# Layer 0 of a four-layer graph kernel: pinned trips through DRAM, reordered small loads, identity products on TensorE, and row scaling on ScalarE

## The chip, the cores and the metric

The kernel runs on one core of one Trainium2 chip. The metric is the device time of one execution in microseconds (us). Every time below is the median of several executions; the profile is one execution, and its span is some 2 us shorter than the time of the same execution (986.9 against 988.83 us before the change). Engines: PE is TensorE's matmul, PEld its weight load, DVE VectorE, ACT ScalarE, POOL GpSimd, SP the engine that issues most DMAs.

## The reference

`x` has 32 batches of 512 nodes with 128 features, `adj` is 512 by 512 with about one entry in eight set. Four layers follow one another, each `x = x + layer(relu(layernorm(x)))`. Only layer 0 matters here:

```python
def _L0_gnn_ref(input, adj, W, e, bias):
    NEG = -9000000000000000.0
    h0 = jnp.einsum('bnf,fg->bng', input, W[0])
    h1 = jnp.einsum('bnf,fg->bng', input, W[1])
    m = adj > 0
    idx = jnp.cumsum(m.reshape(-1).astype(jnp.int32)) - 1
    vals = e[0][idx].reshape(adj.shape)      # e has 256 entries: later ones clamp to the last
    A = jnp.where(m, vals, jnp.float32(NEG))
    A = jax.nn.softmax(A, axis=1)
    M = jnp.eye(adj.shape[0], dtype=A.dtype)
    out = jnp.einsum('ij,bjg->big', A * M, h0) + jnp.einsum('ij,bjg->big', A * (1.0 - M), h1)
    return out + bias[None, None, :]
# ... layers 1 to 3: Chebyshev hops, message passing, attention
```

The comment on `e` is mine: only the first 256 set entries get a value of their own, and the others get the last value, which is why "e's last value" is treated apart.

## The kernel before

The order of instructions on the four computing engines is fixed by the program. The order of DMA issues in SP's queue is not, unless an issue is wrapped in `keep_in_program_order`; a scheduler places the others (in the kernel before, an issue of tile 5 stands in front of tile 4's return, which then comes at 62.91 us). Layer 0 treats the batches in 16 tiles of two. Tiles 0 to 3 are turned to feature-major form by TensorE; from tile 4 on VectorE transposes 32 by 32 squares and the rest of the turn is a trip through DRAM:

```python
    def turn_steps(h, name, done):
        hb = late.tile([P, NQR, 2, NT, QR], F32, tag="hb", name=f"hb_{name}", bufs=2)
        for b in range(2):
            nc.vector.transpose(hb[:, :, b].rearrange("p j t r -> p t j r"),
                                h[:, b].rearrange("p t (j c) -> p t j c", c=QR))
            yield
        d = bounce.tile([NQR, QR, NQR, 2 * P], F32, tag="d", name=f"d_{name}")
        for i in range(NQR):                      # outward: four issues of 128 KB
            nc.sync.dma_start(d[:, :, i, :].rearrange("j c e -> c j e"),
                              hb[i * QR : (i + 1) * QR].rearrange("c j b t r -> c j (b t r)"))
        hT = feature_major(name)                  # return: one issue of 512 KB
        nc.sync.dma_start(hT.rearrange("p i b n -> p (i b n)"), d.rearrange("j c i e -> (j c) (i e)"))
        done[name] = hT
```

The products of a round r (two tiles) are seven; `p_l_a`, `p_l_c` and `p_l_d` are banks of partial sums. Between them stand the projections of the next round's tiles, `p_g`, which read `hT`:

```python
            if i == 0:
                if C + 2 < NQ:
                    go(turn(C + 2))               # round 1: tile 5
            # ...
            elif i == 1:
                if r == 1:
                    go(squares, 3)
                if more:
                    go(projection(A + 2))         # round 1: p_g of tile 4
            # ...
            elif i == 4:
                if r == 1:
                    go(squares, 3)                # its last step: adjT_d, 4 issues of 256 KB
                if A + 4 < NQ:
                    go(turn(A + 4))               # round 1: tile 6
```

(`squares` writes the transposed adjacency to DRAM, where layer 3 reads it.) The start builds the attention matrix from one-hot products:

```python
    def keep_busy(n):                             # products nobody reads: hold the clock up
        p = bank("p_idle")
        for _ in range(n):
            nc.tensor.matmul(p, upto[:, 0, blk(0)], upto[:, 0, :], start=True, stop=True)

    def masked(t):                                # two passes over each row block, on GpSimd
        nc.gpsimd.tensor_scalar(att[:, t, :], m[:, t, :], -2.0 * NEG, NEG, OP.mult, OP.add)
        nc.gpsimd.tensor_scalar(att[:, t, :], att[:, t, :], elastn, None, OP.max)

    def score_rows(t):
        ph = bank(f"p_first_{t}")
        # ... two products at_row x at_col into ph, six at_row x at_part into p_val

    def scaled_rows(t, scaled=None):              # rows 0 to 2: GpSimd; row 3: ScalarE
        if scaled is None:
            nc.gpsimd.tensor_scalar(split(att[:, t, :]), crossed(us[t]), total[:, t : t + 1], None, OP.mult)
        else:
            scaled(split(att[:, t, :]), crossed(us[t]), total[:, t : t + 1])
        # ... diagonal taken out by two more GpSimd operations
```

## Time and profile before

| | before |
|---|---|
| time | 987.59 us (987.29 to 988.96, 3 runs; 987.97 with a fourth) |
| span of the profile | 986.9 us |
| TensorE busy | 961.6 us, 97% |
| TensorE's two waits for a trip through DRAM | 5.84 and 5.78 us |
| first `p_l_a` of round 0 | 33.17 us |

The page, the waits, the two gaps and SP's queue are shown and read in the prediction below. What it only quotes is the start. TensorE's timeline of the kernel before; the columns are start, duration, engine, line, operation, output and inputs, and count, with the idle time before it and its releaser in brackets:

```profile
19.49 0.59 PE L626 MATMUL p_first<-at_col,at_row 128*128 128x512 bf16 x2
19.92 1.74 PE L630 MATMUL p_val<-at_part,at_row 128*128 128x512 bf16 x6
...
28.43 3.74 PE L425 MATMUL p_g<-w,hT 128*128 128x128 f32 x32
...
33.17 1.99 PE L376 MATMUL p_l_a<-g,attT 128*128 128x256 f32 x8
```

The scores begin at 19.49 us, directly behind other products, and the projections of both tiles of round 0 stand together as 32 products after them. Between 9.09 us and `p_l_a` TensorE never idles for more than 0.46 us at a time; in front of 9.09 it had waited 3.56 us for `p_incl`, the first product that needs the whole adjacency.

### The profile page before, as it was taken

Reading aid. Unit: us, or ns where it says so; the run is one execution under the profiler, and the core shown is the slowest. Engines: PE = TensorE matmul, PEld = TensorE weight load, DVE = VectorE, ACT = ScalarE, POOL = GpSimd, SP = SyncE. Lnnn points to the kernel's source line nnn. Section 1 sums busy time; section 2 is a strip of 40 time slices with the busy share of each in tenths; the row PEclk is TensorE's granted clock in tenths of the full one; section 3 lists DMA queues with packets and bytes.
Section 4 is the critical chain, followed back from the end, with each engine's and each line's share of the span. In section 5 each row is a group of like instructions: output and inputs, shape, how many; then the busy total and the mean of one; then the engine's idle time right before and its main releaser. Section 6 shows DMA issues by size and latency. Waiting matters only on the chain.

```text
span 986.9 us, 15155 instructions
## 1 busy us (share of the span) xinstructions
PE 961.6 (97%) x5463; PEld 784.6 (79%) x5464; DVE 578.3 (59%) x1316; ACT 469.9 (48%) x1052; POOL 443.9 (45%) x489
## 2 busy tenths in 40 slices
PE   7977999999999999999999999999999999999998
PEld 3867999989898988989977777777767776777776
DVE  7666787574455456467568665655664444444444
ACT  4762544352421421555836554554664554445553
POOL 7966588855326724421623434444133322233322
PEclk9988999999999999999999999999999999999999
DMA  9046454154232211234332332223132121121111
GB/s 253 10 118 160 129 163 116 43 139 118 68 115 75 65 50 58 76 95 130 86 110 68 122 107 86 69 82 86 43 88 77 51 72 58 54 76 44 54 33 43
DMA packets 83913, 86.04 MB, mean 87 GB/s; under 512 B 6784, under 2 KB 74624, under 8 KB 83840
## 3 DMA queue, kind: packets, MB, share of 16 engines
q1 hardware_dynamic: 83136, 84.96, 30.7%
q8 instruction: 43, 0.70, 0.3%
q14 instruction: 30, 0.25, 0.1%
q10 hardware_dynamic: 704, 0.13, 0.1%
HBM read 44.17 MB, written 40.89 MB: 86 GB/s over the span
## 4 chain that ended last, share of the span: by engine, by line
PE 87%; POOL 4%; DVE 4%; ACT 2%; issue 1%; DMA 1%; SPq 0%; POOLq 0%; DVEq 0%; ACTq 0%
PE p_av L1107 12%; PE p_score L1092 11%; PE p_l_c L376 8%; PE p_l_d L376 5%; PE p_w L425 5%; PE p_l_a L376 5%; PE p_msgT_c L369 4%; PE p_x1T_c L369 4%; PE p_feat L425 3%; PE p_hv L425 3%; PE p_msgT_d L369 3%; PE p_msgT_a L369 3%; PE p_qkh L1079 3%; PE p_l L425 3%; PE p_g L425 3%; PE p_phi L1062 3%
## 5 line engine op out<-in xcount | busy, mean ns | idle before, releaser
L239 ACT ACTIVATE h<-x,sh,rs 128x128 f32<-128x128 f32 x512 | 209.1, 484 | 58.1 <-DVE sh L228 24.7
L1097 POOL TENSOR_TENSOR ex<-ex,adjTx 128x512 f32<-128x512 f32 x64 | 83.3, 1303 | 206.3 <-ACT ex L1095 206.3
L1093 ACT ACTIVATE ex<-p_score 128x512 f32<-128x512 f32 x128 | 71.8, 587 | 124.6 <-issue 113.0
L1107 PEld LDWEIGHTS p_av<-qkh_hv,ex 128*128 128x128 f32 x1024 | 118.5, 191 | 9.4 <-issue 7.4
L1107 PE MATMUL p_av<-qkh_hv,ex 128*128 128x129 f32 x1024 | 120.1, 275 | 0.8 <-POOL ex L1097 0.8
L1092 PE MATMUL p_score<-qkh_hv,hT 128*128 128x512 f32 x256 | 115.2, 593 | 0.0
L275 DVE STREAM_TRANSPOSE hb_hT<-h 128x512 f32<-128x512 f32 x120 | 81.8, 697 | 35.3 <-ACT h L239 34.9
L1097 DVE TENSOR_TENSOR ex<-ex,adjTx 128x512 f32<-128x512 f32 x64 | 45.4, 710 | 81.7 <-ACT ex L1095 81.7
L219 DVE BATCH_NORM_STATS2 bn<-x 128x6 f32<-128x256 f32 x248 | 89.7, 416 | 0.9
L1092 PEld LDWEIGHTS p_score<-qkh_hv,hT 128*128 128x128 f32 x256 | 46.2, 190 | 46.5 <-issue 45.0
L1095 ACT ACTIVATE ex<-ex 128x512 f32<-128x512 f32 x128 | 76.6, 630 | 1.8
L347 POOL TENSOR_TENSOR rt_feat<-feat,feat 128x256 f32<-128x256 f32 x16 | 11.6, 727 | 137.2 <-ACT feat L1046 137.2
L347 POOL TENSOR_TENSOR rt_w<-w 128x512 f32<-128x512 f32 x16 | 20.3, 1269 | 81.1 <-ACT w L953 81.1
L425 PE MATMUL p_w<-th,x1T 128*128 128x128 f32 x256 | 49.5, 275 | 0.0
L425 PE MATMUL p_w<-th,hs 128*128 128x128 f32 x256 | 49.5, 275 | 0.0
L390 ACT COPY x1T<-p_x1T_a 128x256 f32<-128x256 f32 x16 | 5.9, 369 | 84.3 <-PE p_x1T_a L369 84.3
L425 PE MATMUL p_g<-w,hT 128*128 128x128 f32 x256 | 34.7, 294 | 11.6 <-DMA hT<-d_hT 11.6
L425 PEld LDWEIGHTS p_hv<-vw,hT 128*128 128x128 f32 x256 | 33.6, 192 | 15.3 <-issue 8.1
L1057 POOL TENSOR_TENSOR x<-x,phi2b 128x256 f32<-128x256 f32 x64 | 44.5, 728 | 0.0
L450 ACT COPY g<-p_g 128x512 f32<-128x512 f32 x30 | 17.4, 584 | 56.6 <-PE p_g L425 56.4
L425 PEld LDWEIGHTS p_g<-w,hT 128*128 128x128 f32 x256 | 33.4, 209 | 12.6 <-DMA hT<-d_hT 6.2
L1064 ACT ACTIVATE msgT<-p_phi,phi1b 128x512 f32<-128x512 f32 x32 | 21.7, 678 | 40.8 <-PE p_phi L1063 40.8
(230 smaller groups left out, 2104.9 us busy)
## 6 DMA issues: line engine op xcount, KB each, us to landing
d_hT<-hb_hT SPq DMA_DIRECT2D x240, 128.0 KB
hT<-d_hT SPq DMA_DIRECT2D x60, 512.0 KB
x<-in_x_dram SPq DMA_DIRECT2D x32, 256.0 KB
out_dram<-x SPq DMA_DIRECT2D x31, 256.0 KB
adj_s<-in_adj_dram SPq DMA_DIRECT2D x4, 256.0 KB
adjT_d<-adj_squares SPq DMA_DIRECT2D x4, 256.0 KB
sq<-in_adj_dram SPq DMA_DIRECT2D x4, 256.0 KB
adjTx<-adjT_d SPq DMA_DIRECT2D x4, 256.0 KB
```

The source lines that it names most:

```text
L219: nc.vector.bn_stats(st[:, k].rearrange("p e s -> p (e s)"), xt[q][:, b, t : t + 2, :].rearrange("p t f -> p f t"))
L239: nc.scalar.activation(h[:, b, t, :], xt[q][:, b, t, :], AF.Relu, bias=shift[q][:, i : i + 1], scale=scale[q][:, i : i + 1])
L275: nc.vector.transpose(hb[:, :, b].rearrange("p j t r -> p t j r"), h[:, b].rearrange("p t (j c) -> p t j c", c=QR))
L369: nc.tensor.matmul(p[:, :H], b[:, k, :], a[:, k, :], start=(first and k == 0), stop=(k == 1), skip_group_check=True)
L376: nc.tensor.matmul(p[:, i * 2 * D : (i + 1) * 2 * D], a[:, k, blk(i)], b[:, k], start=(first and i == 0 and k == 0), stop=(k == 1), skip_g ...
L425: nc.tensor.matmul(p[:, blk(t)], hT(t), w, start=(i == 0), stop=(i == len(terms) - 1))
L1057: tc.keep_in_program_order(nc.gpsimd.tensor_add(xi, xi, spread(phi2b, 2)))
L1092: nc.tensor.matmul(ps, hT[:, t, b, :], qkh, start=True, stop=True)
L1093: nc.scalar.activation(ex[:, t, :], ps, AF.Tanh, scale=1.0 / (8.0 * math.sqrt(D)))
L1095: nc.scalar.activation(ex[:, t, :], ex[:, t, :], AF.Exp, scale=8.0)
L1097: eng.tensor_mul(split(ex[:, t, :]), split(ex[:, t, :]), crossed(adjTx[0][:, t, :]))
L1107: nc.tensor.matmul(po[:, i, : D + 1], ex[:, t, blk(i0 + i)], hv[:, t, :], start=(t == 0), stop=(t == NT - 1))
```

## The change

Its intent: close the two gaps of nearly 6 us, and shorten the start by relieving GpSimd. The core of the diff (reordered surroundings and renamings are cut):

```diff
# 1. trips of layer 0 keep their order in SP's queue
         d = bounce.tile([NQR, QR, NQR, 2 * P], F32, tag="d", name=f"d_{name}")
+        hT = feature_major(name)
+        held = tc.keep_in_program_order if name.startswith("hT0") else lambda step: step
         for i in range(NQR):
-            nc.sync.dma_start(d[:, :, i, :]...)
-        hT = feature_major(name)
-        nc.sync.dma_start(hT..., d...)
+            held(nc.sync.dma_start(d[:, :, i, :]...))
+        held(nc.sync.dma_start(hT..., d...))
# 2. loads: e, q and k behind x in SP's queue, not in ScalarE's
-    nc.scalar.dma_start(elast, ...)
-    nc.scalar.dma_start(ecol, ...)
-    qw = load_rows(q_w, "qw", nc.scalar)[:, 0, :]
-    kw = load_rows(k_w, "kw", nc.scalar)[:, 0, :]
+    nc.sync.dma_start(ecol, ...)        # behind x of batches 0 to 3, before w0
+    nc.sync.dma_start(elast, ...)
+    qw = load_rows(q_w, "qw")[:, 0, :]
+    kw = load_rows(k_w, "kw")[:, 0, :]
# 3. the mask: one pass, and e's last value by an identity product
-        nc.gpsimd.tensor_scalar(att[:, t, :], m[:, t, :], -2.0 * NEG, NEG, OP.mult, OP.add)
-        nc.gpsimd.tensor_scalar(att[:, t, :], att[:, t, :], elastn, None, OP.max)
+        nc.gpsimd.tensor_scalar(att[:, t, :], m[:, t, :], -1.0, -NEG, OP.add, OP.mult)
+    for t in range(NT):
+        scores[t] = bank(f"p_later_{t}")
+        nc.tensor.matmul(scores[t], ident16, m[:, t, :], start=True, stop=False)
# 4. the ten small operations that split e into three bf16 parts: moved from the
#    front of the program to behind the second next(early[0]) (same code)
# 5. statistics: two of the four small operations to VectorE; tile 1 as a whole
-            nc.gpsimd.tensor_scalar(sd[:, half], st[:, half, :, 2], 1.0 / D, EPS, OP.mult, OP.add)
+            if whole and b == 0:
+                continue
+            half = slice(0 if whole else 2 * b, 2 * b + 2)
+            nc.vector.tensor_scalar(sd[:, half], st[:, half, :, 2], 1.0 / D, EPS, OP.mult, OP.add)
# 6. order on TensorE: the projection of tile 0 before the first scores
-    go(normal[1])
-    go(turned[0])
+    go(normal[1], 3)
+    go(turned[0])
+    next(project[0])
+    go(normal[1])
# 7. ScalarE scales all four row blocks
-            nc.gpsimd.tensor_scalar(split(att[:, t, :]), crossed(us[t]), total[:, t : t + 1], None, OP.mult)
+        nc.scalar.mul(split(att[:, t, :]), crossed(us[t]), total[:, t : t + 1])
# 8. warming products
-    keep_busy(8)
+    keep_busy(16)
# ... keep_busy(3) becomes 4; the later 2, 4 and 1 go; scores, softmax and projections interleave
# ... round 0: the normalising of tile 2 and the statistics behind it move up a little
```

More of the change, by code (lines that the diff above doesn't have):

```diff
@@ L119, in load_x, with load_rows @@
         return nc.sync.dma_start(xt[b // 2][:, b % 2], x[b].rearrange("(t p) f -> p t f", p=P))
-    def load_rows(ap, name, eng=nc.sync):
+    def load_rows(ap, name):
         o = ap.shape[0] // P
         w = const.tile([P, o, ap.shape[1]], F32, name=name)
-        eng.dma_start(w, ap.rearrange("(o f) g -> f o g", f=P))
+        nc.sync.dma_start(w, ap.rearrange("(o f) g -> f o g", f=P))
         return w
@@ L136 @@
         load_x(b)
+    ecol = const.tile([P, NK], F32, name="ecol")
+    nc.sync.dma_start(ecol, e_l0.rearrange("o (k p) -> p (o k)", p=P))
+    elast = const.tile([P, 1], F32, name="elast")
+    nc.sync.dma_start(elast, bass.AP(tensor=e_l0.tensor, offset=e_l0.offset + NE - 1, ap=[[0, P], [1, 1]]))
+    qw = load_rows(q_w, "qw")[:, 0, :]
+    kw = load_rows(k_w, "kw")[:, 0, :]
     w0 = const.tile([P, 2, D], F32, name="w0")
     nc.sync.dma_start(w0, w_l0.rearrange("o f g -> f o g"))
-    elast = const.tile([P, 1], F32, name="elast")
-    nc.scalar.dma_start(elast, bass.AP(tensor=e_l0.tensor, offset=e_l0.offset + NE - 1, ap=[[0, P], [1, 1]]))
-    ecol = const.tile([P, NK], F32, name="ecol")
-    nc.scalar.dma_start(ecol, e_l0.rearrange("o (k p) -> p (o k)", p=P))
-    qw = load_rows(q_w, "qw", nc.scalar)[:, 0, :]
-    kw = load_rows(k_w, "kw", nc.scalar)[:, 0, :]
     b0 = load_bcast(bias_l0, "b0")
@@ L191, in ln_stats, with early_stats @@
             pass
-    def early_stats(q):
+    def early_stats(q, whole):
         st = stats.tile([P, NT, 2, 3], F32, tag="bn", name=f"bn_{q}", bufs=4)
@@ L201, in early_stats @@
         for b in range(2):
-            half = slice(2 * b, 2 * b + 2)
             for k in range(2 * b, 2 * b + 2):
@@ L206, in early_stats @@
                                    xt[q][:, b, t : t + 2, :].rearrange("p t f -> p f t"))
-            nc.gpsimd.tensor_scalar(sd[:, half], st[:, half, :, 2], 1.0 / D, EPS, OP.mult, OP.add)
+            if whole and b == 0:
+                continue
+            half = slice(0 if whole else 2 * b, 2 * b + 2)
+            nc.vector.tensor_scalar(sd[:, half], st[:, half, :, 2], 1.0 / D, EPS, OP.mult, OP.add)
+            nc.vector.tensor_scalar(sh[:, half], st[:, half, :, 1], -1.0, None, OP.mult)
             nc.gpsimd.tensor_tensor(rs[:, half], sd[:, half], minus_half[:, half], OP.pow)
-            nc.gpsimd.tensor_mul(sh[:, half], st[:, half, :, 1], rs[:, half])
-            nc.gpsimd.tensor_scalar(sh[:, half], sh[:, half], -1.0, None, OP.mult)
+            nc.gpsimd.tensor_mul(sh[:, half], sh[:, half], rs[:, half])
             yield
@@ L278, in turn_steps @@
         d = bounce.tile([NQR, QR, NQR, 2 * P], F32, tag="d", name=f"d_{name}")
+        hT = feature_major(name)
+        held = tc.keep_in_program_order if name.startswith("hT0") else lambda step: step
         for i in range(NQR):
-            nc.sync.dma_start(d[:, :, i, :].rearrange("j c e -> c j e"),
-                              hb[i * QR : (i + 1) * QR].rearrange("c j b t r -> c j (b t r)"))
-        hT = feature_major(name)
-        nc.sync.dma_start(hT.rearrange("p i b n -> p (i b n)"), d.rearrange("j c i e -> (j c) (i e)"))
+            held(nc.sync.dma_start(d[:, :, i, :].rearrange("j c e -> c j e"),
+                                   hb[i * QR : (i + 1) * QR].rearrange("c j b t r -> c j (b t r)")))
+        held(nc.sync.dma_start(hT.rearrange("p i b n -> p (i b n)"), d.rearrange("j c i e -> (j c) (i e)")))
         done[name] = hT
@@ L494 @@
     att = square_tile("att")
-    elastn = prep.tile([P, 1], F32, name="elastn")
-    nc.gpsimd.tensor_scalar(elastn, elast, -1.0, None, OP.mult)
-    ecoln = prep.tile([P, NK], F32, name="ecoln")
-    nc.gpsimd.tensor_scalar(ecoln, ecol, -1.0, None, OP.mult)
-    parts = []
-    for i in range(3):
-        eh = prep.tile([P, NK], BF16, name=f"eh_{i}")
-        nc.gpsimd.tensor_copy(eh, ecoln)
-        part = prep.tile([P, NK], F32, name=f"part_{i}")
-        nc.gpsimd.tensor_copy(part, eh)
-        if i < 2:
-            nc.gpsimd.tensor_sub(ecoln, ecoln, part)
-        parts.append(part)
-    keep_busy(8)
+    ident16 = prep.tile([P, P], F16, name="ident16")
+    nc.gpsimd.tensor_copy(ident16, ident)
+    keep_busy(16)
     for t in range(NT):
@@ L513 @@
                                 accum_out=rc[:, t : t + 1])
-    def masked(t):
-        nc.gpsimd.tensor_scalar(att[:, t, :], m[:, t, :], -2.0 * NEG, NEG, OP.mult, OP.add)
-        nc.gpsimd.tensor_scalar(att[:, t, :], att[:, t, :], elastn, None, OP.max)
+        nc.gpsimd.tensor_scalar(att[:, t, :], m[:, t, :], -1.0, -NEG, OP.add, OP.mult)
     rch = prep.tile([P, NT], F16, name="rch")
     nc.vector.tensor_copy(rch, rc)
-    masked(0)
     pi = bank("p_incl")
@@ L529 @@
                              start=(s == 0), stop=(s == t))
-    p = bank("p_qk_t")
-    nc.tensor.transpose(p[:, blk(0)], qw, ident)
-    nc.tensor.transpose(p[:, blk(1)], kw, ident)
-    qkT = prep.tile([P, 2, D], F32, name="qkT")
-    nc.scalar.copy(qkT, tiles(p)[:, :2, :])
-    keep_busy(3)
-    early = [early_stats(q) for q in range(2)]
+    keep_busy(4)
+    early = [early_stats(q, q == 1) for q in range(2)]
     next(early[0])
@@ L546 @@
     nc.vector.tensor_scalar(known[:, :, 0], before, float(NE), None, OP.min)
-    masked(1)
     h = {q: normed_tile(q) for q in range(3)}
@@ L567 @@
                              start=(t == 0), stop=(t == NT - 1))
-    p_qk = bank("p_qk")
-    nc.tensor.matmul(p_qk[:, :D], qkT[:, 0, :], qkT[:, 1, :], start=True, stop=True)
-    keep_busy(2)
     next(early[0])
+    p = bank("p_qk_t")
+    nc.tensor.transpose(p[:, blk(0)], qw, ident)
+    nc.tensor.transpose(p[:, blk(1)], kw, ident)
+    qkT = prep.tile([P, 2, D], F32, name="qkT")
     pgs = prep.tile([P, NT, NE], F16, name="pgs")
@@ L574 @@
     nc.vector.tensor_copy(pgs[:, 2:4, :], pg[1])
+    nc.scalar.copy(qkT, tiles(p)[:, :2, :])
+    elastn = prep.tile([P, 1], F32, name="elastn")
+    nc.gpsimd.tensor_scalar(elastn, elast, -1.0, None, OP.mult)
+    ecoln = prep.tile([P, NK], F32, name="ecoln")
+    nc.gpsimd.tensor_scalar(ecoln, ecol, -1.0, None, OP.mult)
+    parts = []
+    for i in range(3):
+        eh = prep.tile([P, NK], BF16, name=f"eh_{i}")
+        nc.gpsimd.tensor_copy(eh, ecoln)
+        part = prep.tile([P, NK], F32, name=f"part_{i}")
+        nc.gpsimd.tensor_copy(part, eh)
+        if i < 2:
+            nc.gpsimd.tensor_sub(ecoln, ecoln, part)
+        parts.append(part)
     row_of = prep.tile([P, NK], F32, name="row_of")
@@ L579 @@
     nc.vector.tensor_sub(rest, rows[:, :NK], pb[:, :, 0])
-    go(normal[0])
-    next(early[1])
     pw = [bank(f"p_upto_{kk}") for kk in range(NK)]
@@ L586 @@
                              start=(j == 0), stop=(j == NT - 1), skip_group_check=True)
+    p_qk = bank("p_qk")
+    nc.tensor.matmul(p_qk[:, :D], qkT[:, 0, :], qkT[:, 1, :], start=True, stop=True)
+    qk = const.tile([P, D], F32, name="qk")
+    nc.scalar.copy(qk, p_qk[:, :D])
+    scores = {}
+    for t in range(NT):
+        scores[t] = bank(f"p_later_{t}")
+        nc.tensor.matmul(scores[t], ident16, m[:, t, :], start=True, stop=False)
+    go(normal[0])
     copies = [nc.scalar.copy, (nc.scalar.copy, nc.vector.tensor_copy), nc.scalar.copy]
@@ L589 @@
     project = [project_steps(q, hT[q], c) for q, c in ((0, nc.scalar.copy), (1, nc.vector.tensor_copy))]
-    keep_busy(4)
     next(turned[0])
@@ L596 @@
     us = [prep.tile([P, N], F32, tag="u", name=f"u_{t}", bufs=NT) for t in range(NT)]
-    for kk in range(NK):
-        nc.vector.tensor_scalar(at_row[:, kk, :], cols, row_of[:, kk : kk + 1], None, OP.is_equal)
     next(early[1])
@@ L603 @@
                                 accum_out=col_of[:, kk : kk + 1])
-    masked(2)
-    masked(3)
     for kk in range(NK):
+        nc.vector.tensor_scalar(at_row[:, kk, :], cols, row_of[:, kk : kk + 1], None, OP.is_equal)
         nc.vector.tensor_scalar(at_col[:, kk, :], cols, col_of[:, kk : kk + 1], -1.0, OP.is_equal, OP.mult)
@@ L611 @@
                                     parts[i][:, kk : kk + 1], OP.is_equal, OP.mult)
+    go(normal[1], 3)
+    go(turned[0])
+    next(project[0])
     go(normal[1])
-    go(turned[0])
-    qk = const.tile([P, D], F32, name="qk")
-    nc.scalar.copy(qk, p_qk[:, :D])
     diag = prep.tile([P, NT, P], F32, name="diag")
@@ L620 @@
     total = prep.tile([P, NT], F32, name="total")
-    scores = {}
     def score_rows(t):
-        ph = bank(f"p_first_{t}")
+        ph = scores[t]
         for kk in range(NK):
-            nc.tensor.matmul(ph, at_row[:, kk, blk(t)], at_col[:, kk, :], start=(kk == 0), stop=(kk == NK - 1))
+            nc.tensor.matmul(ph, at_row[:, kk, blk(t)], at_col[:, kk, :], start=False, stop=(kk == NK - 1))
         pv = bank(f"p_val_{t}")
@@ L643, in inverse, with scaled_rows @@
         nc.vector.reciprocal(total[:, t : t + 1], total[:, t : t + 1])
-    def scaled_rows(t, scaled=None):
-        if scaled is None:
-            nc.gpsimd.tensor_scalar(split(att[:, t, :]), crossed(us[t]), total[:, t : t + 1], None, OP.mult)
-        else:
-            scaled(split(att[:, t, :]), crossed(us[t]), total[:, t : t + 1])
+    def scaled_rows(t):
+        nc.scalar.mul(split(att[:, t, :]), crossed(us[t]), total[:, t : t + 1])
         own = split(att[:, t, :])[:, :, t, :]
@@ L657 @@
     score_rows(0)
-    keep_busy(1)
-    for t in range(1, NT):
-        score_rows(t)
-    next(turned[1])
     softmax_rows(0)
+    next(project[0])
+    next(project[0])
+    score_rows(1)
     softmax_rows(1)
@@ L665 @@
     scaled_rows(0)
+    score_rows(2)
+    next(turned[1])
     softmax_rows(2)
@@ L668 @@
     scaled_rows(1)
+    score_rows(3)
     next(turned[1])
-    next(project[0])
+    next(turned[1])
     softmax_rows(3)
@@ L673 @@
     scaled_rows(2)
-    next(turned[1])
-    next(project[0])
     go(early_stats_2, 2)
     inverse(3)
-    scaled_rows(3, nc.scalar.mul)
-    next(project[0])
+    scaled_rows(3)
     next(project[1])
@@ L833, in round0 @@
                     nc.scalar.copy(adiag[0], p_adiag)
+                    go(normal[2], NT + 1)
+                    diagonal_of(0, 0)
+                    go(ln3, NT + 1)
                     go(normal[2])
-                    diagonal_of(0, 0)
                     next(left_of_att)
                     next(left_of_att)
-                    go(ln3, NT + 1)
+                    go(ln3)
                 elif i == 2:
@@ L841, in round0 @@
                     add(1, 0, 0)
-                    go(ln3)
                 elif i == 3:
```

## The prediction

> **What bounds the kernel now.** I read the page first: which engine is full, and where its row of tenths is not full.
>
> ```profile
> PE 961.6 (97%) x5463; PEld 784.6 (79%) x5464; DVE 578.3 (59%) x1316; ACT 469.9 (48%) x1052; POOL 443.9 (45%) x489
> PE   7977999999999999999999999999999999999998
> ```
>
> TensorE is busy for 961.6 of 986.9 us, so only about 25 us can be gained without taking work from it. The slices that are not full lie in the first 100 us, and the change touches only layer 0. The order of instructions agrees: with names and line numbers set aside, before and after stand in the same order on every engine from the second round of layer 0 on. So the rest of the span should stay as it is, and I read only the first 110 us closely. TensorE's waits over the whole span:
>
> ```profile
> PE p_g L425 <- DMA hT<-d_hT: 11.6, 2, 5.8
> PE p_incl L528 <- DVE rch L522: 3.6, 1, 3.6
> PE p_x1T_c L369 <- DVE x1T L392: 2.3, 6, 0.4
> ```
>
> (us in total, times, longest.) Two waits for a transposed tile that goes through DRAM make up nearly half of the idle time. The timeline of TensorE around them:
>
> ```profile
> 59.04 1.89 PE L376 MATMUL p_l_c<-rt_g,sums_att 128*128 128x256 f32 x8
> 66.77 3.79 PE L425 MATMUL p_g<-w,hT 128*128 128x128 f32 x16 [5.84 <-DMA hT<-d_hT]
> 70.35 2.92 PE L376 MATMUL p_l_d<-rt_g,sums_att 128*128 128x256 f32 x8
> 73.10 1.89 PE L376 MATMUL p_l_c<-rt_g,attT 128*128 128x256 f32 x8
> ...
> 80.07 1.95 PE L425 MATMUL p_g<-w,hT 128*128 128x128 f32 x16
> 81.85 1.89 PE L376 MATMUL p_l_d<-g,sums_att 128*128 128x256 f32 x8
> ...
> 94.76 3.75 PE L425 MATMUL p_g<-w,hT 128*128 128x128 f32 x16 [5.78 <-DMA hT<-d_hT]
> ```
>
> The reader is to see not only the 5.84 and 5.78 us of waiting, but that the same p_g group takes 3.79 us after a wait and 1.95 us otherwise, and the next group too is long. The windows say why: the granted clock falls to half at about 65.6 us, 4.8 us after TensorE stopped, and is 0.50 until 72.2. The queue that issues the transfers:
>
> ```profile
> 55.11 7.57 SPq L280 DMA_DIRECT2D d_hT<-hb_hT  x5
> 62.91 0.34 SPq L283 DMA_DIRECT2D hT<-d_hT  x1
> 63.30 2.09 SPq L119 DMA_DIRECT2D x<-in_x_dram  x4
> 65.43 2.35 SPq L280 DMA_DIRECT2D d_hT<-hb_hT  x3
> 71.96 0.34 SPq L283 DMA_DIRECT2D hT<-d_hT  x1
> ```
>
> The first row joins four issues for tile 4 and one for tile 5. That fifth waited for VectorE's transpose of tile 5, which ended at 62.35; only then could the return trip of tile 4 be issued. Its outward trip had long landed: the DMA rate is 303 GB/s in the half microsecond from 57.5, 113 in the next, and zero from 58.5. Tile 6 is held in the same way by two issues of tile 7 (d_hT x6 at 82.47 for 7.96 us, return at 90.66).
>
> [...] So an issue whose data is late blocks every later issue of that queue, as the rows above show (4.0 us of blocking for tile 4). [...] e loads issued from ScalarE's queue mix with the adjacency, and would not if they were behind it in SP's queue; in the trace that other queue has 704 packets for only 0.13 MB, and the rate is 64 to 137 GB/s between 2.7 and 3.8 us against 290 later. [...]
>
> **The change, part by part.**
>
> Pinned trips. Tile 4: last outward issue ends at 56.9, data is in at 58.4. A trip without a foreign issue between, tile 8, has its return issued at 110.98, 3.77 us after its first outward issue at 107.21; so tile 4's return would be issued at 55.11 + 3.77 = 58.9. Its data took until about 113.9 for tile 8 (no other transfer in front), 2.9 us, so I take 3.0: landing at 61.9. TensorE needs it when its last p_l_c ends, at 60.8. Wait: 1.1 instead of 5.84. Tile 6: four issues of adjT_d stand before it and share the wires (176 GB/s in the windows), so its outward data is in at 87.4 only; return issued 87.6, landed 90.6, needed at 88.8. Wait: 1.8 instead of 5.78. Gain from waits: 11.6 - 2.9 = 8.7 us.
>
> Clock. The starts of the groups give what the cold clock cost: p_g 66.77 to 70.35 is 3.58 against 80.07 to 81.85, 1.78; p_l_d 2.75 against 1.73: together 2.8 us. The second time p_g 3.55 and p_l_d 2.43 (starts 94.76, 98.31, 100.74): 2.5 us. With waits of 1 to 2 us both go: 5.3 us.
>
> Tile 5 and tile 7 now follow the loads of x in the queue: 1 MB at about 310 GB/s, 3.3 us, then 0.5 MB outward and the return of 3.0: landed near 70.6, needed 10.4 us after tile 4's p_g, at 72.4. Still hidden, with under 2 us in hand.
>
> Start. In the kernel before, the first product of round 0 (p_l_a) starts at 33.17, paced by GpSimd, whose last four items per row block are scale 1.57, diagonal 0.46, subtract 0.46. Three scales (4.7 us) go to ScalarE, where the fourth took 0.72. The mask pairs on GpSimd (0.62 + 1.57, four times) become one early pass of 0.62 each; the maximum with e's last value becomes four identity products of 128x512 f16, near 0.22 each at full clock. The adjacency, whose four parts were taken up at 4.68, 5.66, 6.76 and 7.68, should be complete about 0.9 us earlier: an estimate, from the rates above. Sixteen warming products instead of eight should let the p_row products run at 0.11 in place of 0.21 each; only the last four of these lie on the path: 0.4 us.
>
> But something new stands on the path. TensorE's order now has the p_g of tile 0 before the first score products. It waits for ScalarE's two hT copies, these for three normalising activations of tile 1, these for GpSimd's power, and that stands behind the ten small operations that split e, which used to run from 4.9 to 8.3 us beside the adjacency's load. With the 0.9 taken off: statistics of tile 0's second half 13.5, power 14.7, shift 15.0, ten operations at 0.26 each 17.6, power of eight columns 1.2 to 1.9 (four took 1.16) 19.1, shift 19.4, three activations 20.7, copies 21.8, second half of p_g 23.1. Then four score groups of 1.73, p_hT 0.87, p_g 1.79, attention transposes 0.9, a copy of 0.5: 34.1. That is 0.9 later than 33.17, although GpSimd is relieved. In round 0 the wait of 1.1 us before the second p_hT (45.62) is ScalarE's and shrinks by some 0.2 through the earlier shift of tile 3. Start: +0.7.
>
> Sum: -8.7 - 5.3 + 0.7 = -13.3; 987.6 - 13.3 = 974.3.
>
> **The rivals.** (a) A new wait takes the place: if the return trips take 3.9 us, as both did before with pieces of the next tile in front, or if tiles 5 and 7 come late behind x, waits of 2 to 3 us each remain, perhaps with a cold clock: 979 to 982. The slack of under 2 us speaks for it; the four later rounds, which have the pinned order already and show no wait, against. (b) The start gains rather than loses: if the short GpSimd operations finish in shorter time or scores don't really wait on them, freeing GpSimd of 4.7 us brings p_l_a to 31, the total to 970 or 971. (c) Everything is hidden anyway because TensorE is 97% busy: then 985. Against it: TensorE is without a gap after 100 us, so an arrival of the second p_g some 13 us earlier goes through to the end undiminished.
>
> **Range and chances.** The gaps carry most: 14 us, give or take 2.5. The start is my least certain part, +0.7 give or take 2. Together 969 to 979. Faster by over 2% means below 967.8, which needs both gaps shut and a start 2 us shorter: 0.06. Slower by over 2%: 0.01. Within 2%: 0.93.
>
> **What would show it.** In the changed profile: p_g's waits for hT under 2.5 us each; the p_g group after them near 1.95; the granted clock 1.00 from 60 to 100; the return trip of tile 4 issued before any issue of tile 5; p_l_a of round 0 starting between 31 and 36; the last part of the adjacency taken up near 6.8. The prediction is wrong if the clock still falls to half, if tile 5 or 7 makes a wait, or if the first score product starts far from 23.

## The result and the profile after

The changed kernel takes 980.12 us (979.82 to 980.45, 4 runs) against 987.97 us (987.29 to 988.96, 4 runs). The ratio is 0.992, with a 95% interval of 0.9903 to 0.9937. All ratios here are the mean time of one kernel's fast runs over that of the other's fast runs of the same rounds, so not quite the ratio of the medians. The change is a gain of 0.8%. The time lies 1.1 us above the upper end of the predicted range and 5.8 us above the predicted value. Between the medians the gain is 7.85 us, between the two profiles below 9.0 us: the profiled execution of the kernel before took 988.83 us, 0.9 us more than its median.

The page of the changed kernel, the rows that answer to those of before:

```profile
PE 959.3 (98%) x5470; PEld 782.7 (80%) x5470; DVE 578.5 (59%) x1322; ACT 471.5 (48%) x1055; POOL 430.1 (44%) x473
PE   7998999999999999999999999999999999999998
```

The third and fourth slices have filled up. The waits of TensorE (total, times, longest):

```profile
PE p_g L428 <- DMA hT<-d_hT: 4.3, 2, 2.8
PE p_g L428 <- ACT hT L262: 3.5, 1, 3.5
```

The DRAM waits shrank from 11.6 to 4.3 us, and a wait of 3.5 us that did not exist before has come. TensorE's timeline says where:

```profile
14.89 1.53 PE L259 MATMUL p_hT<-ident,h 128*128 128x128 f32 x8
19.95 3.78 PE L428 MATMUL p_g<-w,hT 128*128 128x128 f32 x16 [3.54 <-ACT hT L262]
23.53 1.06 PE L622 MATMUL p_later<-at_col,at_row 128*128 128x512 bf16 x2
24.38 1.89 PE L626 MATMUL p_val<-at_part,at_row 128*128 128x512 bf16 x6
26.11 0.59 PE L622 MATMUL p_later<-at_col,at_row 128*128 128x512 bf16 x2
...
35.51 1.99 PE L379 MATMUL p_l_a<-g,attT 128*128 128x256 f32 x8
...
64.30 2.05 PE L428 MATMUL p_g<-w,hT 128*128 128x128 f32 x16 [1.50 <-DMA hT<-d_hT]
...
86.56 3.65 PE L428 MATMUL p_g<-w,hT 128*128 128x128 f32 x16 [2.76 <-DMA hT<-d_hT]
```

Three `p_g` groups of 16 equal products stand here. The one behind the 1.50 us wait takes 2.05 us; those behind 3.54 and 2.76 us take 3.78 and 3.65. The windows of the same stretch show the reason (columns: window, its length, busy time and count of PE, PEld, DVE, ACT and POOL, then the granted TensorE clock, the DMA share and GB/s):

```profile
18.50:19.00 0.50, 0.00 (x0) 0.00 (x0) 0.50 (x2) 0.50 (x3) 0.00 (x0) 0.50 1.18 294
...
86.00:86.50 0.50, 0.00 (x0) 0.00 (x0) 0.50 (x3) 0.00 (x0) 0.50 (x2) 1.00 1.09 325
86.50:87.00 0.50, 0.44 (x2) 0.47 (x3) 0.50 (x3) 0.00 (x0) 0.50 (x1) 0.69 0.73 212
87.00:87.50 0.50, 0.50 (x4) 0.50 (x4) 0.50 (x3) 0.00 (x0) 0.50 (x2) 0.50 0.98 267
```

The clock is 0.50 in the new hole of the start, and it falls to 0.50 again at the end of the second wait: TensorE stopped at 83.80 and resumed at 86.56, and the halving came at 86.69. The queue of SP after the change:

```profile
56.98 1.78 SPq L284 DMA_DIRECT2D d_hT<-hb_hT  x4
60.80 0.34 SPq L286 DMA_DIRECT2D hT<-d_hT  x1
61.19 2.08 SPq L119 DMA_DIRECT2D x<-in_x_dram  x4
64.25 1.83 SPq L284 DMA_DIRECT2D d_hT<-hb_hT  x4
...
73.87 3.37 SPq L481 DMA_DIRECT2D adjT_d<-adj_squares  x4
77.28 3.64 SPq L284 DMA_DIRECT2D d_hT<-hb_hT  x4
83.02 0.34 SPq L286 DMA_DIRECT2D hT<-d_hT  x1
```

The pin works: tile 4's return stands directly behind its own four outward issues, and tile 5's follow later. For tile 6 another thing remains in front: the four issues of `adjT_d`, 1 MB that nobody needs soon. Behind them even the issuing of tile 6's four pieces takes 3.64 us instead of 1.78.

Set side by side, with the two profiles cut at the same instructions:

| step | predicted | measured |
|---|---|---|
| start, up to `p_l_a` of round 0 (33.17 → 35.51) | +0.9 | +2.34 |
| rest of round 0, to the last `p_l_c` before the first wait (27.76 → 27.29) | −0.2 | −0.47 |
| first wait, tile 4 (5.84 → 1.50) | −4.74 | −4.34 |
| clock behind it, `p_g` and `p_l_d` by starts (6.33 → 3.62) | −2.8 | −2.71 |
| second wait, tile 6 (5.78 → 2.76) | −3.98 | −3.02 |
| clock behind it, the same two groups (5.98 → 5.22) | −2.5 | −0.76 |
| sum | −13.3 | −8.96 |

The spans differ by 986.9 − 977.9 = 9.0 us, so the table leaves nothing over: beyond it the two kernels run alike. The 4.3 us that are missing lie in three rows: 1.4 in the start, 1.0 in the second wait and 1.7 in the clock behind it; smaller differences of the other rows make up the rest.

### The profile page after: what moved, and what is told of

Read it like the earlier page. It is cut to its first block, busy times and chain, and to the rows that moved or that the text cites.

```text
span 977.9 us, 15160 instructions
## 1 busy us (share of the span) xinstructions
PE 959.3 (98%) x5470; PEld 782.7 (80%) x5470; DVE 578.5 (59%) x1322; ACT 471.5 (48%) x1055; POOL 430.1 (44%) x473
## 4 chain that ended last, share of the span: by engine, by line
PE 89%; DVE 4%; ACT 3%; DMA 2%; POOL 1%; issue 1%; SPq 0%; DVEq 0%; ACTq 0%; POOLq 0%
PE p_av L1100 12%; PE p_score L1085 11%; PE p_l_c L379 8%; PE p_l_a L379 5%; PE p_l_d L379 5%; PE p_w L428 5%; PE p_msgT_c L372 4%; PE p_x1T_c L372 4%; PE p_feat L428 3%; PE p_hv L428 3%; PE p_g L428 3%; PE p_msgT_d L372 3%; PE p_msgT_a L372 3%; PE p_qkh L1072 3%; PE p_l L428 3%; PE p_phi L1055 3%
## 5 line engine op out<-in xcount | busy, mean ns | idle before, releaser
L350 POOL TENSOR_TENSOR rt_feat<-feat,feat 128x256 f32<-128x256 f32 x16 | 11.6, 725 | 137.3 <-ACT feat L1039 137.3
L1105 DVE SCALAR_TENSOR_TENSOR x<-p_av,rsum,x 128x128 f32<-128x128 f32 x128 | 39.1, 347 | 1.9
```

## The experiments

My theory after the result: (1) pinning alone gives the whole gain and more; (2) the start loses about 2 us, because the projection of tile 0 was put ahead of the scores and opens a hole in which the clock halves; (3) the second wait is made by `adjT_d`, and its length lies just where the clock may or may not halve. The rivals: the other parts (loads, identity products, ScalarE's scaling) bear the loss or a gain of their own; the hole itself and not the clock is what costs; and moving `adjT_d` only moves the wait to another tile. Twelve kernels were run, all correct, each timed in five rounds against the kernel before on the same chip (before: 987.4, 988.6 and 988.05 us).

**Pinning alone** (the kernel before with part 1 of the diff and nothing else).

```diff
+        held = tc.keep_in_program_order if name.startswith("hT0") else lambda step: step
-            nc.sync.dma_start(d[:, :, i, :]...)
+            held(nc.sync.dma_start(d[:, :, i, :]...))
-        nc.sync.dma_start(hT..., d...)
+        held(nc.sync.dma_start(hT..., d...))
```

> The kernel before with only the pinned order of layer 0's trips. Theory A (the start of the changed kernel loses about 2 us, and the pinning alone is worth more than the whole change): the two waits fall from 5.8 us each to 1.5 and 2.8, the first no longer halves the clock (2.8 us), the second still does for one group (1.7 of 2.5 us left), so about -4.3 -2.8 -3.0 -0.8 = -10.9 us, near 977, some 3 us faster than the changed kernel. Rival B (the start is neutral and the pinning gives all of the measured gain): 980, the same as the changed kernel. p_l_a of round 0 should start at 33.2 as before.

Measured: 977.8 us (976.22 to 978.16), ratio 0.9897. That is faster than the whole change (0.992): its slowest execution is 1.7 us below the fastest of the changed kernel, though the two intervals just touch (0.991 and 0.9903). Its timeline:

```profile
33.03 1.99 PE L377 MATMUL p_l_a<-g,attT 128*128 128x256 f32 x8
...
62.26 2.05 PE L426 MATMUL p_g<-w,hT 128*128 128x128 f32 x16 [1.47 <-DMA hT<-d_hT]
...
84.42 2.02 PE L426 MATMUL p_g<-w,hT 128*128 128x128 f32 x16 [2.66 <-DVE bn L219]
```

The start stays at 33.03, the first wait is 1.47 us. The second is 2.66 us, as long as in the whole change, but in this execution `p_g` behind it ran in 2.02 us: the clock held. (The releaser named there, VectorE, is the one the profile puts last; the transfer is its likely partner.) So the pin is the gain, and the other parts together cost some 2 us; the next run checks this from the other side.

**All but the pin** (the changed kernel with the pin taken out).

```diff
-        held = tc.keep_in_program_order if name.startswith("hT0") else lambda step: step
+        held = lambda step: step
```

> The changed kernel with the pinned order taken back. Theory A: the waits of 5.8 us and the cold groups return (+10.9), so 991, 2 to 3 us slower than the kernel before: that is what the new start costs. Rival B (start neutral): 988, the time of the kernel before. p_l_a of round 0 should start at 35.5 as in the changed kernel.

Measured: 989.94 us (988.06 to 991.14), ratio 1.0022. The waits are back at 5.79 and 5.66 us, and `p_l_a` starts at 35.53. The rest of the change makes the kernel slower by 0.1 to 0.35% (the interval is 1.001 to 1.0035), about 2 us, which is what the start lost.

**Scores before the projection** (the changed kernel; one line moved).

```diff
     go(turned[0])
-    next(project[0])
     go(normal[1])
 ...
     score_rows(0)
+    next(project[0])
     softmax_rows(0)
```

> The changed kernel with the p_g of tile 0 put behind the first row block's score products in TensorE's order. Theory A (this p_g, which waits 3.5 us for ScalarE's copy of tile 0, stands in front of the scores and lets the clock halve): the scores start near 17 instead of 23.5, TensorE is not idle over 1 us there, p_g takes 1.95 instead of 3.78; p_l_a of round 0 starts some 3.5 us earlier and the whole near 976.6. Rival C (the scores wait for VectorE and ScalarE anyway, above all exp behind the normalising of tile 1): under 1 us of gain, 979.5.

Measured: 975.57 us (974.0 to 976.89), ratio 0.9877. In its timeline:

```profile
17.15 0.90 PE L621 MATMUL p_later<-at_col,at_row 128*128 128x512 bf16 x2 [0.22 <-DVE at_col L604]
...
20.47 2.05 PE L428 MATMUL p_g<-w,hT 128*128 128x128 f32 x16 [0.48 <-ACT hT L262]
...
31.75 1.99 PE L379 MATMUL p_l_a<-g,attT 128*128 128x256 f32 x8
```

The scores need nothing that `p_g` waits for. They start at 17.15 instead of 23.53, the hole shrinks from 3.54 to 0.48 us, `p_g` runs at full clock, and `p_l_a` comes 3.8 us earlier. When the adjacency is complete varies between executions, so the start is better counted from `p_incl`: `p_l_a` follows it after 28.43 us in the changed kernel, after 24.18 us here, after 24.08 us in the kernel before and after 24.54 us with pinning alone. The loss in the start, 4.3 us counted in this way, is this one line. Against the kernel before, the other parts show no gain behind `p_incl`; what they gain lies in front of it (`p_incl` at 7.57 here, at 9.09 before).

**The same hole, filled** (the changed kernel; products that nobody reads fill the idle time).

```diff
     go(turned[0])
+    keep_busy(16)
     next(project[0])
```

> The changed kernel with 16 idle products between the transposes of tile 0 and its p_g, which fill the 3.5 us of waiting and change no wait. If the halved clock is a cost of its own: p_g takes about 1.95 instead of 3.78 and the first score group 0.4 less, so p_l_a starts about 2.3 us earlier and the time is near 977.8. If the softmax chain on VectorE and ScalarE paces the start regardless of the clock: within 0.7 us of 980.1.

Measured: 978.76 us (976.29 to 981.26), ratio 0.9909. The hole is still there, for TensorE's useful work still waits for ScalarE's copies, but the clock is up:

```profile
21.59 2.05 PE L428 MATMUL p_g<-w,hT 128*128 128x128 f32 x16
```

In this execution everything before was late (`p_incl`, the first product that needs the whole adjacency, ended its wait at 8.68 us against 7.08 in the changed kernel). Counted from there `p_l_a` starts after 34.60 − 8.68 = 25.92 us instead of 35.51 − 7.08 = 28.43: 2.5 us earlier. Two other profiles with the hole unfilled and the start unchanged have 27.34 (all but the pin) and 27.51 (`adjT_d` behind tile 6), so the price of the cold clock alone is 1.4 to 2.5 us. The time agrees with it (1.4 us below the changed kernel) but doesn't show it alone, for the intervals of the two ratios overlap. The second wait was 2.69 us in this profile and halved the clock (`p_g` 3.53).

**`adjT_d` behind tile 6** (the changed kernel; two statements exchanged).

```diff
-                if r == 1:
-                    go(squares, 3)
                 if A + 4 < NQ:
                     go(turn(A + 4))
+                if r == 1:
+                    go(squares, 3)
```

> The changed kernel with the write of the transposed adjacency moved behind tile 6's trip in the queue. If the four adjT_d issues (1 MB at 176 GB/s) in front of tile 6 are what leaves 2.8 us of waiting there: tile 6's return is issued some 5 us sooner relative to TensorE, the second wait is gone (under 0.3 us) and with it the chance of a halved clock: -2.8 us, -4.4 in executions where the clock halved, so 975.8 to 977.4. Rival D (tile 6 is late because VectorE's transpose of it is late, or tile 7 now becomes late behind the adjacency): the wait stays or moves to tile 7, 980.

Measured: 979.69 us (976.3 to 979.82), ratio 0.9901 (0.9888 to 0.9914): the interval overlaps with that of the changed kernel.

```profile
83.67 1.95 PE L428 MATMUL p_g<-w,hT 128*128 128x128 f32 x16
...
96.66 3.55 PE L428 MATMUL p_g<-w,hT 128*128 128x128 f32 x16 [2.35 <-DMA hT<-d_hT]
```

Tile 6's wait has gone, and tile 7 waits 2.35 us instead: its trip now stands behind both `adjT_d` and the loads of x. The rival was right here: the megabyte stands before whichever trip comes next. That a wait of only 2.35 us halved the clock I had not expected.

**Scores first and `adjT_d` behind tile 6, together** (the two edits already shown).

```diff
-    next(project[0])              # before the scores
+    next(project[0])              # behind score_rows(0)
-                if r == 1:        # before turn(A + 4)
-                    go(squares, 3)
+                if r == 1:        # behind turn(A + 4)
+                    go(squares, 3)
```

> The changed kernel with the scores first and the adjacency's write behind tile 6: both repairs. If the two losses are independent: 975.6 of the scores-first kernel less 2.6 us (its second wait), near 973, faster than all others. If something else takes over in the second round (tile 7, GpSimd's differences), 975.6.

Measured: 974.97 us (973.96 to 976.32), ratio 0.9863. Tile 7 waits 3.09 us in the profile, yet `p_g` behind it takes 2.02 us: the clock held through a longer wait than the one that halved it in the run before. How the two waits lay is shown below, in what the runs say about the clock.

**e, q and k loaded by ScalarE's queue again** (the changed kernel with part 2 undone).

```diff
-    nc.sync.dma_start(ecol, ...)
-    nc.sync.dma_start(elast, ...)
-    qw = load_rows(q_w, "qw")[:, 0, :]
-    kw = load_rows(k_w, "kw")[:, 0, :]
+    nc.scalar.dma_start(elast, ...)
+    nc.scalar.dma_start(ecol, ...)
+    qw = load_rows(q_w, "qw", nc.scalar)[:, 0, :]
+    kw = load_rows(k_w, "kw", nc.scalar)[:, 0, :]
```

> The changed kernel with the e, q and k loads back on ScalarE's queue beside the adjacency. If they slow the adjacency as the rates of the kernel before suggest: its last part is taken up 1.5 us later (about 7.6 instead of 6.1) and everything behind it too, 981.6. Rival E (the adjacency comes early for another reason or its gain is hidden behind the path over GpSimd's power): within 0.5 us of 980.1.

Measured: 980.62 us (978.87 to 981.51), ratio 0.9915: the intervals of this ratio and that of the whole change overlap. The last part of the adjacency was taken up at 7.60 us. Over all profiles, kernels with these loads in ScalarE's queue show 7.54 to 7.68 (three), those with them in SP's show 5.99 to 7.72 (eleven, mean 6.85): earlier by about 0.8 on average, but not in each execution. The first `p_l_a` came at 36.27, 0.76 us later than in the changed kernel. The time fits rival E (within 0.5 us of 980.1); what part 2 is worth the times don't resolve.

**Rows 0 to 2 scaled by GpSimd again** (the changed kernel with part 7 undone).

```diff
-        nc.scalar.mul(split(att[:, t, :]), crossed(us[t]), total[:, t : t + 1])
+        if t < 3:
+            nc.gpsimd.tensor_scalar(split(att[:, t, :]), crossed(us[t]), total[:, t : t + 1], None, OP.mult)
+        else:
+            nc.scalar.mul(split(att[:, t, :]), crossed(us[t]), total[:, t : t + 1])
```

> The changed kernel with the scaling of row blocks 0 to 2 back on GpSimd (1.57 us each instead of 0.71 on ScalarE). Theory F (in the new order the end of the start is set by TensorE and the last row's exp, not by GpSimd, so the relief of GpSimd is worth nothing): within 0.7 us of 980.1, p_l_a at 35.5 or earlier because ScalarE has less to do. Rival G (GpSimd would still pace it, as in the kernel before): p_l_a 1.5 us or more later, 981.7.

Measured: 981.74 us (978.15 to 983.95), ratio 0.9929. Counted from `p_incl` (7.95), `p_l_a` starts 28.31 us later, as in the changed kernel (28.43). In both profiles the clock was halved for 6.83 us in the hole, so they can be compared: the first `p_l_a` hardly depends on who scales. The time itself lies near the 981.7 of rival G, but the six executions are 5.8 us apart and the interval (0.9914 to 0.9945) overlaps with that of the changed kernel, so the time decides nothing. Behind `p_l_a` 0.5 us were lost up to the first wait (27.83 us against 27.29), with `p_l_c` waiting 0.61 us for an eviction, and the first wait was 2.32 us. Behind this wait the clock fell late:

```profile
66.50:67.00 0.50, 0.50 (x5) 0.50 (x6) 0.50 (x2) 0.06 (x1) 0.50 (x2) 1.00 0.98 263
67.00:67.50 0.50, 0.50 (x7) 0.50 (x6) 0.50 (x2) 0.00 (x0) 0.50 (x1) 1.00 0.92 257
67.50:68.00 0.50, 0.50 (x5) 0.50 (x4) 0.50 (x2) 0.39 (x1) 0.50 (x1) 0.52 0.86 243
```

TensorE had resumed at 66.41 and was busy throughout these windows; the clock halved at 67.52, 1.1 us after the wait had ended.

**`adjT_d` put off by a round, with the scores first** (the third experiment, and the last step of `squares` moved from round 1 to round 2, behind the trip of tile 7).

```diff
             if i == 0:
                 if C + 2 < NQ:
                     go(turn(C + 2))
+                if r == 2:
+                    go(squares)
 ...
             elif i == 4:
                 if r == 1:
-                    go(squares, 3)
+                    go(squares, 1)
```

> The scores-first kernel with the write of the transposed adjacency moved once more, behind the trip of tile 7 (the run before moved the wait from tile 6 to tile 7). If the 1 MB only needs a place with enough slack: no wait at tiles 6 and 7, tile 8 still hidden, no clock change after the first 20 us; 975.6 less 2.6 us, 972.9. If the wait only moves on to tile 8: 975.

Measured: 972.21 us (971.33 to 972.42), ratio 0.9838 (0.9825 to 0.9851): level with a variant of it below, it is the fastest of all, and it beats both the kernel before and the changed one. Its timeline:

```profile
59.72 2.05 PE L428 MATMUL p_g<-w,hT 128*128 128x128 f32 x16 [1.34 <-DMA hT<-d_hT]
...
98.70 2.02 PE L428 MATMUL p_g<-w,hT 128*128 128x128 f32 x16 [0.25 <-DMA hT<-d_hT]
```

Tile 6's four issues now take 1.75 us, its return follows 3.71 us after the first, and its wait is gone. `adjT_d` stands before tile 8, whose wait is 0.25 us. The granted clock is 1.00 in all four executions, and their times lie within 1.1 us.

**e split earlier** (the changed kernel; the ten small GpSimd operations moved up, behind the first half of tile 0's statistics).

```diff
     next(early[0])
+    elastn = ...      # the ten operations, unchanged
+    ecoln = ...
+    for i in range(3): ...
 ...
     next(early[0])
-    elastn = ...
-    ecoln = ...
-    for i in range(3): ...
```

> The changed kernel with GpSimd's ten small operations on e put in front of tile 0's second half, where GpSimd stood idle from 9.4 to 12.4 us. If these ten stand on the path to tile 0's p_g as the prediction had it: the power of tile 1 starts about 1.3 us sooner, p_g waits some 2.2 us instead of 3.5, and the clock may hold; 977.5 to 979. If e is not landed by 10 us, GpSimd waits for it and nothing is gained: 980.

Measured: 977.43 us (976.47 to 977.95), ratio 0.9891. GpSimd waited 0.74 us for e, yet the power for tile 1 (the element-wise power in its statistics, 128x8 elements) came 1.3 us earlier counted from `p_incl` (7.68 us behind it against 8.99), and the hole shrank:

```profile
19.72 2.05 PE L428 MATMUL p_g<-w,hT 128*128 128x128 f32 x16 [2.05 <-ACT hT L262]
```

With 2.05 us instead of 3.54 the clock held, and `p_l_a` starts at 32.73, 24.43 us behind `p_incl` instead of 28.43. This shows the cause of the hole: what the copies of `hT` wait for is GpSimd's chain of small operations. The second wait was 2.69 us and halved the clock.

**`adjT_d` put off, scores first, and e split earlier** (the last two experiments together).

```diff
+    elastn = ...      # the ten operations at the earlier place
-    next(project[0])  # before the scores
+    next(project[0])  # behind score_rows(0)
+                if r == 2:
+                    go(squares)       # behind turn(C + 2)
-                    go(squares, 3)
+                    go(squares, 1)
```

> The kernel of the first run of this set with the ten operations on e early as well. With the scores first TensorE waits only 0.5 us for tile 0's copy, so at most that is left: 972.4 to 973, the same as the first run within 0.5 us.

Measured: 972.04 us (971.59 to 972.54), ratio 0.9838: the same as without the second part. With the scores first `p_g` waits only 0.48 us for `hT`, so an earlier `hT` buys nothing that the times show.

**Without the identity products** (the changed kernel; two mask operations per row block on GpSimd, in a stretch where it idles).

```diff
-        nc.gpsimd.tensor_scalar(att[:, t, :], m[:, t, :], -1.0, -NEG, OP.add, OP.mult)
-        nc.tensor.matmul(scores[t], ident16, m[:, t, :], start=True, stop=False)
+    for t in range(NT):
+        nc.gpsimd.tensor_scalar(att[:, t, :], m[:, t, :], -2.0 * NEG, NEG, OP.mult, OP.add)
+        nc.gpsimd.tensor_scalar(att[:, t, :], att[:, t, :], elastn, None, OP.max)
 ...  (the first score product then starts its bank: start=(kk == 0))
```

> The changed kernel with the identity products taken out and the two mask operations per row block back on GpSimd, in its idle stretch from 18.1 to 30.3 us. If the identity products save nothing here because TensorE and VectorE wait at that time anyway: within 0.5 us of 980.1. If the 8.8 us of mask operations come to stand in front of the softmax (the first att is needed near 24.6): 1 us or more slower, 981 to 982.

Measured: 982.35 us (980.52 to 982.89), ratio 0.9939. The time is near the second outcome of the expectation, but not for its reason. In the start `p_l_a` comes at 35.74, 0.2 us later, and counted from `p_incl` as in the changed kernel (28.36 us against 28.43); the first wait is 1.37 us. The rest of the loss lies at the second wait, 3.46 us, with both groups behind it cold: tile 6's return was issued at 83.85, 6.47 us after its first outward issue, against 5.74 in the changed kernel. Why that trip took 0.7 us longer stays open; I have one profile of it, and nothing in this part of the program differs. So the profile shows no gain by the identity products in the start, and the difference of about 2 us behind it is not explained. Parts 5 (statistics) and 8 (warming products) of the diff were not run alone.

### What the runs say together about the clock

Each execution comes with the mean granted clock of its core. Within one kernel, on one chip, it sorts the times:

| kernel | spans of its executions, us (mean granted clock) |
|---|---|
| scores before the projection | 972.2 (1.000), 971.9 (1.000), 974.6 (0.998), 974.7 (0.998) |
| that, and `adjT_d` behind tile 6 | 971.8 (1.000), 972.5 (1.000), 973.2 (1.000), 974.2 (0.998) |
| `adjT_d` put off by a round | 969.2, 970.1, 970.1, 970.3 (all 1.000) |

A clock of 0.998 over 972 us means 1.9 us of missing clock, or about 3.9 us at half speed: by estimate one cold stretch (in the changed kernel the two took 6.83 and 3.41 us); the executions that had it are 2.4 to 2.8 us longer in the first kernel and 1.0 to 2.4 us in the second. So the same program is cold in some executions and not in others. Nor does the length of a wait decide it. Of the waits of `p_g` in the profiles, those of 2.32, 2.35, 2.61, 2.69, 2.71 and 2.76 us had the clock halved, others of 2.05, 2.61, 2.66 and 3.09 us had not; none of 1.7 us or less had, and each of 3.46 us or more had.

More can be read from the traces. In the kernel before the clock rises at 14.39 us, halves at 65.59, rises at 72.41, halves at 92.89 and rises at 99.72: distances of 15, 2, 6 and 2 times 3.413. In the changed kernel it rises at 4.77, halves at 18.42, rises at 25.25, halves at 86.69 and rises at 90.10: distances of 4, 2, 18 and 1 times 3.413. Where these times lie differs between the two profiles. With steps of 3.413 us, laid in each trace from its own clock changes, as windows, TensorE's busy time in each is (columns: window, its length, busy time and count of PE, granted clock, DMA share and GB/s; first two windows of the changed kernel, then two of scores first with `adjT_d` behind tile 6):

```profile
15.01:18.42 3.41, 1.35 (x9) 1.00 1.16 294
83.27:86.69 3.42, 0.66 (x4) 1.00 0.75 229
89.06:92.47 3.41, 1.72 (x12) 1.00 0.41 109
92.47:95.89 3.42, 2.02 (x17) 1.00 0.58 200
```

| wait | idle in each window of 3.413 us that it touches | clock behind it |
|---|---|---|
| changed kernel, 2.76 us | 2.76 | halved at the window's end |
| e on ScalarE's queue, 2.61 us | 2.55, rest in the window behind | halved at the window's end |
| scores first, 2.61 us | 1.23 and 1.39 | held |
| pinning alone, 2.66 us | 1.94 and 0.73 | held |
| scores first and `adjT_d` behind tile 6, 3.09 us | 1.70 and 1.40 | held |

The two traces of the change, before and after, have 563 such windows at full clock. In six of them TensorE idled for 2.06 us or more (three in each trace, the last at the end of the program), and the clock halved at the end of each of the six. In the others it idled for 1.50 us at most, and the clock did not halve. (Counted from the first rise of the clock on; before it the traces have no record.) Together with the table: of these windows, those with 1.94 us of idle time or less kept the clock, and those with 2.06 us or more lost it. So the wait of 3.09 us, cut in two, kept it, and that of 2.61 us with 2.55 us in one window did not. In the run with rows 0 to 2 scaled by GpSimd the 2.31 idle us lay in the window 64.11 to 67.52, and the clock fell at its end, when TensorE had already resumed. In the kernel before, both waits of nearly 6 us held a window without any product (62.17 to 65.59 and 89.48 to 92.89), so these two could not tell how much less is enough.

## Why the prediction was right or wrong

**The unchanged rest, right.** The whole difference of the spans lies in the six rows of the table, all before 94 us. TensorE passed an earlier arrival through to the end undiminished, as the prediction argued from its share of 97%.

**The pin, right in mechanism.** Tile 4's return was issued 3.82 us after its first outward issue (predicted 3.77, taken from tile 8), before any issue of tile 5, and the first wait was 1.50 us (predicted 1.1), for the return took 3.5 us to the product that reads it, not 3.0. The clock behind it stayed up and gave 2.71 us (predicted 2.8). Tiles 5 and 7 came in time, so the rival of a late tile behind x fell. Pinning alone and its counterpart show both sides of it.

**The start, wrong.** The step that failed: "three activations 20.7, copies 21.8, second half of p_g 23.1. Then four score groups of 1.73". The sum came near (the scores start at 23.53), but from wrong terms. GpSimd's chain was quicker: the power for the second half of tile 0 starts at 12.39 and the ten small operations are done at 16.1,

```profile
12.39 1.01 POOL L211 TENSOR_TENSOR rs<-sd,minus_half 128x4 f32<-128x4 f32 x1 [3.02 <-DVE sh L210]
...
13.64 0.23 POOL L556 TENSOR_SCALAR elastn<-elast 128x1 f32<-128x1 f32 x1
...
16.07 1.78 POOL L211 TENSOR_TENSOR rs<-sd,minus_half 128x8 f32<-128x8 f32 x1
```

(GpSimd's timeline of the changed kernel) so `p_g` started at 19.95. Against that, TensorE now idled for 3.54 us, the clock halved at 18.42, `p_g` took 3.58 us instead of the 1.78 of a warm one, and the first score group 2.58 instead of 1.73. The prediction had the hole on paper, from the end of `p_hT` to 21.8, and it had read the halved clock behind both waits of the kernel before; it reckoned with it only where the change removes a wait, and not where its own walk put a new one. Filling the hole (−1.4 to −2.5 us) and putting the scores first (−4.3 us, both counted from `p_incl`) show this: the rest of the 4.3 us goes with the idle time itself. The range of the start, give or take 2, did hold its +2.34, but with luck: counted from `p_incl` the start lost 4.35 us (24.08 to 28.43), and in this profile `p_incl` came 2.0 us earlier than before (7.08 against 9.09), where 0.9 had been expected. The other changed starts with e in SP's queue have `p_incl` at 7.15 to 8.68.

**The second wait, its size off.** Predicted 1.8 us, measured 2.76. The return was issued at 83.02, 0.78 us before TensorE needed the tile, where the prediction had 1.2 us before; and it took 3.5 us to `p_g`, where 3.0 had been assumed. The prediction did count `adjT_d` in front, but took 8.55 us from its first issue to tile 6's return (79.05 to 87.6), and it took 9.15 us (73.87 to 83.02). The 3.0 us had been read from tile 8, to the last data and not to the product; in the profiles of the changed kernel and of pinning alone it is 3.45 to 3.54 us to the product for tiles 4 and 6. Together 1.0 us.

**The clock behind the second wait, wrong.** The step: "With waits of 1 to 2 us both go". It was my estimate; the kernel before had shown the halved clock only behind two waits of nearly 6 us (the 4.8 us after the last product are 4.7 in the trace), and not what a shorter wait does. In the changed kernel 2.06 us of idle time in one window of 3.413 us were enough. With 1.8 us of waiting the clock would have held, an estimate from the windows with up to 1.94 us of idle time, which kept it. The 2.76 us fell into one window, and the clock was lost: 0.76 us gained of 2.5. Three of the four executions of the changed kernel have the profile's mean clock of 0.995 (the fourth 0.996), so it was no single bad profile. Putting `adjT_d` off by a round removes the wait, and with it the chance.

**The rivals.** The prediction's rival (a), waits of 2 to 3 us that keep a cold clock, "979 to 982", is what came at the second wait, though through `adjT_d` and not through x. Rival (b), that relieving GpSimd brings `p_l_a` to 31 us, seems to come true with the scores first (31.09 to 32.11 in three profiles), but not by its cause: counted from `p_incl` these starts take 23.94 to 24.18 us, and the kernel before took 24.08. The gain lies in front of `p_incl`. Rival (c) fell.

**The small parts.** The adjacency is complete about 0.8 us earlier on average (predicted 0.9); between 2.7 and 3.8 us the DMA rate is 311 GB/s in the changed kernel and 103 in the kernel before. The identity products gained nothing that the start shows. The `p_row` products, expected at 0.11 us each after more warming products, took 2.75 us for the 16, against 3.38 before. ScalarE's scaling moved nothing before `p_l_a` in the changed order; what it is worth without the hole was not run alone.

## What to carry to other kernels

When you walk through a changed order on paper, note how long each engine idles in the new walk, and look at the clock there too: the hole that this reordering opened brought 3.54 us of idle time and then a `p_g` of 3.58 us that takes 1.78 warm. Of the windows of 3.413 us read here, those with 1.94 us of idle time or less kept the clock, and those with 2.06 us or more lost it. Put first on TensorE what needs nothing from a long chain: here that was worth 4.3 us. When you pin a trip in a queue, look at what still stands in front of it: a transfer that nobody needs soon belongs behind the ones that are waited for. Tile 6's four issues took 3.64 us behind 1 MB of `adjT_d`, and 1.75 us without it. Take the length of a trip up to the product that waits for it: out and back were 3.82 + 3.50 us for tile 4, where I had reckoned with 3.77 + 3.0 from one other trip. And read from a trace what an operation takes on its engine: GpSimd's power took 1.01 to 1.20 us for 128x4 elements and 1.64 to 1.80 us for 128x8, while a product of the same size mostly took 0.20 to 0.26 us.
